# Filter row sums by accumulating transfers, input parts of a convolution in steps, and a projection's first products in other PSUM tiles

## The chip, the cores and the metric

The kernel runs on one core of a Trainium2 chip. The metric is the device time of one execution in microseconds. TensorE (PE) multiplies, with PEld for its weight loads; VectorE (DVE) works elementwise; ScalarE (ACT) applies functions and copies; GpSimd (POOL) does small work and issues DMAs; SyncE (SP) issues DMAs alone.

## The reference

Eight images of 512 channels and 32 x 32 points go through one residual block. All is float32.

```python
def cbs(x, w, p, pad):
    return silu(bn_eval(conv2d(x, w, pad), p))

def bot_attention(x, qkv_w, rw, rh):             # 4 heads of 64 channels, 1024 positions
    q, k, v = conv2d(x, qkv_w, 0) split in three
    logits = einsum('bhdi,bhdj->bhij', q, k + (rw + rh)) * 64 ** -0.5
    return einsum('bhij,bhdj->bhdi', softmax(logits), v)

t = cbs(group_norm(x), cv1_w, cv1_bn, 0)         # 512 -> 512, 32 groups
ys = [t[:, :256], t[:, 256:]]
for i in range(2):
    yi = ys[-1]
    z = cbs(yi, m_cv1_w[i], m_cv1_bn[i], 1)      # 3 x 3, 256 -> 256
    z = bot_attention(z, m_qkv_w[i], m_rw[i], m_rh[i])
    ys.append(yi + silu(bn_eval(conv2d(z, m_cv2_w[i], 0), m_cv2_bn[i])))
out = x + cbs(concatenate(ys), cv2_w, cv2_bn, 0) # 1024 -> 512
```

## The kernel before

**Stages.** The images go through in four pairs (a and b). A pair runs: input tiles and 3 x 3 convolution of module n=0 for both images, projection and attention of a, projection and attention of b, then the same for n=1, then cv2. The group norm and cv1 of the next pair run inside these attentions and between them. Pair 0 has no pair before it: its norm and cv1, and those of image 2, run at the start.

**The 3 x 3 convolution** uses a minimal-filtering (Winograd) scheme with rows and columns transformed apart. `conv3x3` (L585) makes six turns (two output blocks, three row groups i), each with an inner and an outer PSUM tile of the pool `big` (three tiles). VectorE combines them: two instructions form m from the inner tile (L649, L650), one e from the outer tile (L652), and more follow. In the last turn this is done image by image ("parts"), so that part 0's silu comes early. `first_sum` (L872) gives t1 for the projection.

**Filters.** `make_u` (L393) transforms one block of 3 x 3 filters, nine taps of 128 x 128 in `area`, into 18 tiles, in eight steps on VectorE (a generator; every `next` makes a step): for i=2 two column steps; for i=0 a row step (L400 to L402) and two column steps; for i=1 a row step (L404 to L406) and two column steps. ScalarE copies the outer columns, POOL stores the results. The blocks of module 0 are made at the start; those of module 1 in pair 0: one in `early`, in the projection of a, and the others by `step_u` in and around the two attentions. `load_late` brings their taps through POOL's queue into the padded images Y2, which are idle then.

**Input tiles.** `tiles_in` (L513) transforms a padded image for one i in twelve VectorE instructions, with two memsets on POOL for the edges. For n=1 the tiles of image a are made early: i=1 and i=2 by `tiles_later` in attention b of n=0 (i=1 before it in pairs 0 to 2), stored by POOL into `v_dram` and loaded by SP before the convolution.

**Projection.** `project_strassen` (L875) forms q, k and v with seven products instead of eight, each of two q/k matmuls (512 columns) and four for v, into the pools `big` (three tiles) and `av` (one). Fourteen projections use it; seven of them follow a convolution directly, the other seven pass `early` (sums of the attention before). Pair 0's n=0 uses `project_direct` (L827), where VectorE adds the position terms to k from PSUM (L845, L846).

**Attention.** `attention_fast` (L975) takes four groups (channel block, half) of eight key blocks, in pairs. Per pair TensorE makes logits (L998), ScalarE the exponentials (L1002), TensorE the values (L1032), VectorE adds the exponentials up (L1016, L1018) for the sums (L1049). At a group's end ScalarE and VectorE evict the one `av` tile into z (L1039, L1040). Other work hangs on the pairs: `behind` maps a key (group, pair), or the group alone for its pair 0, to functions, which `hooks` builds from norm steps, `step_u` steps and extras. Key (0,3) stands behind the eviction of group 0; the later group ends have no such edge.

**Order.** A planner orders the instructions of each engine: of those that are ready in its model, the one traced first goes first. `tc.issue_after(ins)` puts what is traced under it behind `ins`, on the engine of `ins` alone. Engines and queues are then strictly in order. PSUM dependences are kept by tile: a write to one half waits for a reader of the other.

**Pair 0's extras.** In attention a: twelve `step_u` steps, the position sums of module 1 (`make_r`, L202: a ScalarE turn and four VectorE sums of 128 x 512, each stored by POOL) and the weight sums of its projection (`make_sq`, L234: four sums of 128 x 384 and seven POOL stores). In attention b: eight `step_u` steps and `tiles_later(2)` at (2,1).

Of the kernel before, what the change touches and what calls it, by code (L numbers as in the profile page):

```python
# [61 lines left out]
def kernel(  # L62
# [70 lines left out]

    def load_taps(n, oc, k, area):
        nc.sync.dma_start(
            area[:, : 9 * P].rearrange("p (t o) -> p t o", o=P), m_cv1_w[n, ts(k, P), :, ts(oc, P)]
        )
        return area
# [254 lines left out]
    def make_u(n, oc, k, area, full=None, new=u_new_late, stores=None):  # L393
# [4 lines left out]
        for i in (2, 0, 1):  # L398
            if i == 0:
                tt(mid[:, 1], g0, g2, ALU.add)  # L400
                tt(mid[:, 0], mid[:, 1], g1, ALU.add)
                last = tt(mid[:, 1], mid[:, 1], g1, ALU.subtract)  # L402
            elif i == 1:
                stt(mid[:, 1], g2, 4.0, g0, ALU.mult, ALU.add)  # L404
                stt(mid[:, 0], g1, 2.0, mid[:, 1], ALU.mult, ALU.add)
                last = stt(mid[:, 1], g1, -2.0, mid[:, 1], ALU.mult, ALU.add)  # L406
# [67 lines left out]
    def stages(act, small, ps_big, ps_av, n_pt):  # L474
# [38 lines left out]
        def tiles_in(yp, put, is_=(0, 1, 2), ec=None, room=None, ec_at=("rs", 4)):  # L513
# [17 lines left out]
            for i in is_:  # L531
                ba = g = None
                if i == 0:
                    ba = row_tile("w_ba")
                    stt(ba, rows(1, 2), -4.0, rows(3, 2), ALU.mult, ALU.add)
                elif i == 1:
                    for j in range(2):
                        ec[j] = act.tile([P, NT, NM * F], F32, tag=ec_at[0], name="w_ec", bufs=ec_at[1])
                        tt(ec[j], rows(3 + j)[:, :, 0], rows(1 + j)[:, :, 0], ALU.subtract)
                else:  # L540
                    g = row_tile("w_g")
                    tt(g, rows(0, 2, 5), rows(2, 2), ALU.subtract)
# [6 lines left out]
                if i == 0:  # L549
                    tt(to[0], two(ba[:, :, 1]), two(ba[:, :, 0]), ALU.add)  # L550
                    tt(to[1], two(ba[:, :, 1]), two(ba[:, :, 0]), ALU.subtract)
                elif i == 1:
                    stt(to[0], two(ec[0]), 2.0, two(ec[1]), ALU.mult, ALU.add)
                    stt(to[1], two(ec[0]), -2.0, two(ec[1]), ALU.mult, ALU.add)
                else:
                    stt(to[0], two(ec[1]), 0.25, two(g[:, :, 0]), ALU.mult, ALU.add)
                    stt(to[1], two(ec[0]), -4.0, two(g[:, :, 1]), ALU.mult, ALU.add)
# [14 lines left out]
                tt(d_of(2), cols(M0 + 1, M1 - M0), cols(M2, M3 - M2), ALU.subtract)  # L572
# [3 lines left out]
                stt(v34[:, 1], d[:, 1], -2.0, d[:, 2], ALU.mult, ALU.add)  # L576
# [5 lines left out]
                last = tt(v12[:, 1], a, b, ALU.subtract)  # L582
            return last

        def conv3x3(n, vs, u_of, z, groups=G, summed=None, after=None, between={}):  # L585
# [10 lines left out]
            for oc in range(NM):  # L596
                dst = z[:, oc].rearrange("p g x -> p (g x)").rearrange("p (t r w) -> p r t w", r=4, w=F)
                for i in range(NI):
# [44 lines left out]
                    m_t = m.rearrange("p r a q -> p (r a q)")  # L643
                    for part in range(parts):
                        qs, tl, xs_ = ts(part, n_q), ts(part, n_q // NT), ts(part, 4 * n_q)
                        m = m_t.rearrange("p (g r a q) -> p g r a q", a=4, **by_part)[:, part]
                        e = e_t.rearrange("p (g r a q) -> p g r a q", a=2, **by_part)[:, part]
                        r = r_t.rearrange("p (g r t x s) -> p g r t x s", g=parts, r=2, x=4, s=NT)[:, part]
                        tt(m[:, :, 0::2], slots(inner_ps, 0)[..., qs], m24[..., qs], ALU.add)  # L649
                        tt(m[:, :, 1::2], slots(inner_ps, 0)[..., qs], m24[..., qs], ALU.subtract)  # L650
# [224 lines left out]
        def project_strassen(n, z, w, t, early=None, middle=None):  # L875
# [10 lines left out]
            def product(ps, v, w, rhs, onto=False, between=None):  # L886
# [4 lines left out]
                if between:  # L891
                    between()
                for j in range(HALF // P):
# [3 lines left out]
                    )  # L897

# [18 lines left out]
            ps_a, ps_b, ps_v = big(), big(), ps_av.tile([P, 2, HALF], F32, tag="av", name="pv_ps")  # L917
# [3 lines left out]
            product(ps_a, ps_v[:, 0], w["11"], b11, between=early)  # L921
            nc.scalar.copy(u, ps_a)
            nc.scalar.copy(u_v, ps_v[:, 0])
            product(ps_b, ps_v[:, 1], w["s1"], t1)
            nc.scalar.copy(m5, ps_b)  # L925
# [644 lines left out]
    chunk = make_u(0, 0, 0, areas[0, 0, 0], first_units)  # L1570
# [19 lines left out]
    chunk = make_u(0, 0, 1, areas[0, 0, 1], first_units, stores=first_stores)  # L1590
# [9 lines left out]
    with tc.issue_after(made.ins), tc.issue_after(powered.ins):  # L1600
        nc.vector.tensor_scalar(rstd, bnp[:, :, 3], BN_EPS, None, ALU.add)
        nc.gpsimd.tensor_tensor(rstd, rstd, mhalf[:, :NBN], ALU.pow)
# [13 lines left out]
    norm = s.group_norm_part(xs_second, by_act=NX - 1, behind=behind_u)  # L1616
# [78 lines left out]

    def third_norm(done):
        with tc.issue_after(last.ins), tc.issue_after(s.silued[0].ins), tc.issue_after(done.ins):
            next(norm)

    def third_parts(done):  # L1700
        for g in range(G):
            s.tiles_in(Y1[g], putter(vs, g), [2], ecs[g])

# [9 lines left out]
    for p in range(NP):  # L1713
# [57 lines left out]
        def load_late(oc, k, area):  # L1771
            nc.gpsimd.dma_start(
                area[:, : 9 * P].rearrange("p (t o) -> p t o", o=P), m_cv1_w[1, ts(k, P), :, ts(oc, P)]
            )
            return area

# [5 lines left out]
        if p == 0:  # L1782
            with tc.issue_after(powered.ins):
                first_taps, second_taps = [load_late(0, k, inside(Y2[k])) for k in range(NM)]
# [19 lines left out]
        if direct:  # L1804

            def early():
                with tc.issue_after(s.silued[0].ins):
                    for _ in make_u(1, 0, 0, first_taps, new=u_new_early):
# [43 lines left out]
        if p == 0:  # L1852
            more_u = filters([(0, 1, second_taps), (1, 0, load_late(1, 0, inside(Y2[0])))])
            late_taps = []
# [4 lines left out]
            extra = {key: lambda: next(r_steps) for key in ((0, 3), (1, 1), (1, 3), (2, 1), (2, 3))}  # L1859
            extra[2, 2] = lambda: late_taps.append(load_late(1, 1, inside(Y2[1])))  # L1860
            
            def with_sq():
                with tc.issue_after(put_r[0].ins):
                    make_sq(1, q_tiles, [t[:, j] for t in q_sums for j in range(2)])

            extra[3, 2] = with_sq
        behind = hooks(() if p == 0 else NORM_A, {i: 1 for i in range(12)}, extra) | {NG: begin_cv1(0, Y1[0], ia + 2)}
# [41 lines left out]
        else:  # L1909
# [11 lines left out]
            if direct:  # L1921
                m2_a()
                end.check()
                with tc.issue_after(s.m2_silu[0].ins):
# [297 lines left out]
```

## Time and profile before

| | us |
|---|---|
| three runs | 2284.47, 2286.85, 2290.32 (median 2286.85) |
| profiled execution | 2286.45, of which the span is 2284.6 |
| PE / DVE / ACT / POOL busy in the span | 2218.8 / 1753.0 / 1097.9 / 204.7 |
| mean granted TensorE clock | 0.993 |
| moved by DMA | 281.06 MB, 123 GB/s |

The span runs from the first instruction to the last. A wait is the idle time of an engine ahead of an instruction, put down to what released it: "who <- whom: us in total, times, longest". A row of a stage gives its bounds in us, its length, the busy time (and number of instructions) of the engines, the granted clock, and the share and rate of DMA.

### The profile page before, as it was taken

Reading aid. Unit: us, or ns where it says so; the run is one execution under the profiler, and the core shown is the slowest. Engines: PE = TensorE matmul, PEld = TensorE weight load, DVE = VectorE, ACT = ScalarE, POOL = GpSimd, SP = SyncE. Lnnn points to the kernel's source line nnn. Section 1 sums busy time; section 2 is a strip of 40 time slices with the busy share of each in tenths; the row PEclk is TensorE's granted clock in tenths of the full one; section 3 lists DMA queues with packets and bytes.
Section 4 is the critical chain, followed back from the end, with each engine's and each line's share of the span. In section 5 each row is a group of like instructions: output and inputs, shape, how many; then the busy total and the mean of one; then the engine's idle time right before and its main releaser. Section 6 shows DMA issues by size and latency. Waiting matters only on the chain.

```text
span 2284.6 us, 40531 instructions
## 1 busy us (share of the span) xinstructions
PE 2218.8 (97%) x16338; PEld 1081.3 (47%) x16338; DVE 1753.0 (77%) x2701; ACT 1097.9 (48%) x1361; POOL 204.7 (9%) x409
## 2 busy tenths in 40 slices
PE   7999999999999999999999999999999999999997
PEld 3653437343474444734447343654345643473443
DVE  7988789878668689886857868986784868886742
ACT  7454553554225665366324666455622455336533
POOL 2212010000220000000021000000012000000002
PEclk9999999999999999999999999999999999999999
DMA  7835247321572323612267151532137611251115
GB/s 256 297 127 192 75 140 261 108 74 57 138 241 86 106 90 107 206 53 75 56 162 254 32 176 33 176 118 77 55 80 180 215 53 46 69 195 43 47 29 135
DMA packets 128420, 281.06 MB, mean 123 GB/s; under 512 B 34112, under 2 KB 56364, under 8 KB 127200
## 3 DMA queue, kind: packets, MB, share of 16 engines
q1 hardware_dynamic: 100240, 192.25, 25.7%
q0 software_dynamic: 27984, 86.13, 12.6%
q8 instruction: 131, 2.15, 0.4%
q14 instruction: 65, 0.53, 0.1%
HBM read 210.29 MB, written 68.03 MB: 122 GB/s over the span
## 4 chain that ended last, share of the span: by engine, by line


## 5 line engine op out<-in xcount | busy, mean ns | idle before, releaser
L1002 ACT ACTIVATE pt<-l_ps 128x1024 f32<-128x1024 f32 x512 | 495.6, 1023 | 363.1 <-PE l_ps L998 332.7
L1018 DVE TENSOR_TENSOR acc<-acc,pt 128x1024 f32<-128x1024 f32 x384 | 469.8, 1223 | 94.2 <-ACT pt L1002 71.9
L1032 PE MATMUL av_ps<-pt,vT 64*64 64x512 f32 x4096 | 491.3, 597 | 15.1 <-DVE z L1040 14.8
L998 PE MATMUL l_ps<-q,kr 64*64 64x512 f32 x4096 | 487.2, 592 | 1.7 <-ACT pt L1002 0.8
L1032 PEld LDWEIGHTS av_ps<-pt,vT 64*64 64x64 f32 x4096 | 155.8, 134 | 291.2 <-issue 240.0
L998 PEld LDWEIGHTS l_ps<-q,kr 64*64 64x64 f32 x4096 | 158.5, 134 | 274.5 <-issue 253.5
L628 PEld LDWEIGHTS c_ps<-v_in,u 128*64 128x64 f32 x4320 | 235.7, 137 | 5.3 <-issue 5.3
L628 PE MATMUL c_ps<-v_in,u 128*64 128x128 f32 x4320 | 237.5, 273 | 0.0
L1231 PE MATMUL m_ps<-z,m_sb 128*128 128x512 f32 x256 | 112.8, 593 | 0.4 <-DVE z L1104 0.4
L633 ACT COPY c_m<-c_ps 128x512 f32<-128x512 f32 x48 | 28.2, 587 | 175.9 <-PE c_ps L628 130.3
L888 PE MATMUL p_ps<-t_z,sq 128*128 128x512 f32 x224 | 108.1, 602 | 3.2 <-DVE c_t L650 3.2
L1016 DVE TENSOR_TENSOR acc<-pt 128x1024 f32<-128x1024 f32 x64 | 78.0, 1218 | 34.3 <-ACT pt L1002 34.3
L478 ACT ACTIVATE t<-m_ps,bh,sh 128x512 f32<-128x512 f32 x64 | 46.4, 775 | 87.8 <-PE m_ps L1231 87.8
L888 PE MATMUL p_ps<-z,sq 128*128 128x512 f32 x168 | 80.8, 604 | 0.2 <-ACT m_z L925 0.2
L1301 POOL DMA_DIRECT2D c_out<-in_x_dram x56 | 49.9, 975 | 310.1 <-ACT c_out L478 307.8
L1231 PEld LDWEIGHTS m_ps<-z,m_sb 128*128 128x128 f32 x256 | 48.2, 190 | 59.6 <-issue 56.4
L1104 DVE TENSOR_TENSOR z<-z,rs 128x512 f32<-128x512 f32 x64 | 43.9, 686 | 23.6 <-DMA rs<-r_dram 23.1
L478 ACT ACTIVATE c_out<-cz,bh,sh 128x512 f32<-128x512 f32 x14 | 16.7, 1295 | 90.3 <-DVE cz L1328 90.3
L1040 DVE TENSOR_TENSOR z<-av_ps,z 128x512 f32<-128x512 f32 x64 | 44.0, 688 | 19.5 <-ACT z L1039 19.5
L478 ACT ACTIVATE z<-z,bh,sh 128x512 f32<-128x512 f32 x64 | 47.7, 805 | 22.0 <-DVE z L677 22.0
L888 PEld LDWEIGHTS p_ps<-t_z,sq 128*128 128x128 f32 x224 | 39.2, 192 | 35.8 <-issue 35.8
L1351 PE MATMUL x_ps<-t_x,sw 128*128 128x512 f32 x128 | 55.9, 592 | 0.0
(308 smaller groups left out, 3163.1 us busy)
## 6 DMA issues: line engine op xcount, KB each, us to landing
u<-u SPq DMA_DIRECT2D x135, 512.0 KB
sq<-sq SPq DMA_DIRECT2D x42, 384.0 KB
rs<-r_dram SPq DMA_DIRECT2D x118, 128.0 KB
x<-in_x_dram SPq DMA_DIRECT2D x28, 512.0 KB
r_in<-r SPq DMA_DIRECT2D x28, 512.0 KB
y_in<-y SPq DMA_DIRECT2D x28, 512.0 KB
c_out<-in_x_dram POOLq DMA_DIRECT2D x56, 256.0 KB, 5.4
out_dram<-c_out POOLq DMA_DIRECT2D x56, 256.0 KB, 3.8
```

Of the source, the lines that this page charges most:

```text
L478: silued[0] = nc.scalar.activation(dst, src, AF.Silu, scale=sh[:, k : k + 1], bias=bh[:, k : k + 1])
L628: conv_product[0] = nc.tensor.matmul(to[o], us[cp][:, k, row, c, o], rhs, start=(k == 0), stop=(k == NM - 1),)
L888: nc.tensor.matmul(ps[:, o, :], w[:, o, :], rhs, start=not onto, stop=True, skip_group_check=onto)
L998: nc.tensor.matmul(ps[kh * HD : (kh + 1) * HD, hd, :], kr[r, c, o : o + HD], q[r, c, ts(half, HALF)], start=True, stop=True,)
L1002: last_exp[0] = exp = nc.scalar.activation(pt, ps, AF.Exp, scale=SCALE)
L1016: return nc.vector.tensor_tensor(accs[g], pt[0], pt[1], ALU.add)
L1018: ins = nc.vector.tensor_tensor(accs[g], accs[g], pt[i], ALU.add)
L1032: nc.tensor.matmul(avs[g][hd * HD : (hd + 1) * HD, kh, :], vT[r, j, o : o + HD], pt[i][r, hd, :], start=(j == 0), stop=(j == NJ - 1),)
L1040: evicted[0] = nc.vector.tensor_tensor(dst, av[:, 1], dst, ALU.add)
L1231: nc.tensor.matmul(pss[half][:, oc, :], m2_sb[:, n, k, ts(oc, P)], ao[:, k, ts(half, HALF)], start=(k == 0), stop=(k == NM - 1),)
L1301: nc.gpsimd.dma_start(t, rows_of(x, i, at), accum_op=ALU.add)
L1351: nc.tensor.matmul(ps[:, o, :], w[:, c, ts(o, P)], rhs[c], start=(c == 0 and not onto), stop=(c == 1), skip_group_check=onto,)
```

## The change

- `make_u` takes a switch `summed`. With it (all but the first two blocks), g0+g1+g2 of a block's taps is expected in the area's rows 9 to 11, and i=0's row step is one instruction in place of three. The sum is made by DMA: `load_row` brings tap row r there, row 0 plainly, rows 1 and 2 with `accum_op=ALU.add`. For the two blocks (0,1,k), row 0 goes through SP and rows 1 and 2 through POOL, behind the power of `rstd`. For module 1, `load_late` issues taps and three rows on POOL; its first two calls move from before the first convolution to the hook `third_parts` in it, behind the power of the third image's statistics.
- The statistics of image 1's fourth chunk are made by ScalarE instead of VectorE (`by_act=NX`).
- `tiles_in` becomes a generator of five pieces (`tiles_steps`). In attention b of n=0 a piece each is made at (1,3), (2,1), (2,3), 3 and (3,2); in pair 3 the ten pieces of i=1 and i=2 are made at the keys (g,1) to (g,3).
- In the last turn of `conv3x3` the m instructions of both parts come before the rest.
- In `project_strassen` ps_b is the `av` tile and ps_v a `big` tile; both q/k products come first, then the two v products, and the copies in another order.
- In pair 0, attention a keeps ten `step_u` steps and the ScalarE turn; the four position sums, the weight sums and five steps of block (1,1) come behind m2 of image a, before the projection of b. Attention b keeps three steps.

```diff
+    def load_row(n, oc, k, area, r, q=None, **kw):
+        (q or nc.gpsimd).dma_start(
+            area[:, 9 * P : 12 * P].rearrange("p (t o) -> p t o", o=P),
+            m_cv1_w[n, ts(k, P), 3 * r : 3 * r + 3, ts(oc, P)], **kw
+        )
...
             if i == 0:
-                tt(mid[:, 1], g0, g2, ALU.add)
-                tt(mid[:, 0], mid[:, 1], g1, ALU.add)
-                last = tt(mid[:, 1], mid[:, 1], g1, ALU.subtract)
+                if summed:
+                    last = stt(mid[:, 1], g1, -2.0, mid[:, 0], ALU.mult, ALU.add)
...
+                    for part in range(parts):
+                        qs, m = ts(part, n_q), m_parts[:, part]
+                        tt(m[:, :, 0::2], slots(inner_ps, 0)[..., qs], m24[..., qs], ALU.add)
+                        tt(m[:, :, 1::2], slots(inner_ps, 0)[..., qs], m24[..., qs], ALU.subtract)
                     for part in range(parts):
...
-            ps_a, ps_b, ps_v = big(), big(), ps_av.tile([P, 2, HALF], F32, tag="av", name="pv_ps")
+            ps_a, ps_b, ps_v = big(), ps_av.tile([P, 2, HALF], F32, tag="av", name="p_ps"), big()
...
-            product(ps_a, ps_v[:, 0], w["11"], b11, between=early)
+            to_qk(ps_a, w["11"], b11)
+            if early:
+                early()
+            to_qk(ps_b, w["s1"], t1)
+            to_v(ps_v[:, 0], w["11"], b11)
             nc.scalar.copy(u, ps_a)
+            nc.scalar.copy(m5, ps_b)
+            to_v(ps_v[:, 1], w["s1"], t1)
             nc.scalar.copy(u_v, ps_v[:, 0])
-            product(ps_b, ps_v[:, 1], w["s1"], t1)
-            nc.scalar.copy(m5, ps_b)
             nc.scalar.copy(m5_v, ps_v[:, 1])
...
+        scaled = nc.gpsimd.tensor_tensor(rstd, rstd, mhalf[:, :NBN], ALU.pow)
+        with tc.issue_after(scaled.ins):
+            for r in (1, 2):
+                for k in range(NM):
+                    load_row(0, 1, k, areas[0, 1, k], r, accum_op=ALU.add)
...
-    norm = s.group_norm_part(xs_second, by_act=NX - 1, behind=behind_u)
+    norm = s.group_norm_part(xs_second, by_act=NX, behind=behind_u)
...
+        for r in range(3):
+            load_row(1, oc, k, area, r, **({"accum_op": ALU.add} if r else {}))
...
+        with tc.issue_after(after_norm[0].ins):
+            late_taps.extend(load_late(0, k, inside(Y2[k])) for k in range(NM))
...
-            extra = {key: lambda: next(r_steps) for key in ((0, 3), (1, 1), (1, 3), (2, 1), (2, 3))}
-            extra[2, 2] = lambda: late_taps.append(load_late(1, 1, inside(Y2[1])))
...
+            extra = {
+                (2, 2): lambda: late_taps.append(load_late(1, 1, inside(Y2[1]))), (3, 1): lambda: next(r_steps),
+            }
+        behind = hooks(() if p == 0 else NORM_A, {0: 2} | {i: 1 for i in range(1, 9)}, extra) | {NG: begin_cv1(0, Y1[0], ia + 2)}
...
-                m2_a()
+                last = m2_a()
                 end.check()
+                with tc.issue_after(last.ins):
+                    for _ in r_steps:
+                        pass
+                    with tc.issue_after(put_r[0].ins):
+                        make_sq(1, q_tiles, [t[:, j] for t in q_sums for j in range(2)])
+                more_u = filters([(1, 1, late_taps[2])])
+                with tc.issue_after(last.ins):
+                    for _ in range(5):
+                        step_u()
...
+        parts_at = iter(())
+        if more:
+            parts_at = tiles_later(2)
+        else:
+            parts_at = (part for i in (1, 2) for part in tiles_later(i))
...
+        at_keys = ((1, 3), (2, 1), (2, 3), 3, (3, 2)) if more else [(g, at) if at else g for g in range(NG) for at in range(1, 4)]
+        behind = hooks(NORM_B, {0: 1, 1: 1, 4: 1}, {key: step_part for key in at_keys}) | {
...
-        apply = behind[2, 1]
-        behind[2, 1] = lambda: (apply(), tiles_later(2))
```

## The prediction

> **What bounds the kernel now.** I read the page's busy times first, then TensorE's waits, then each attention as a stage of its own, then single stalls on the timeline.
>
> ```profile
> span 2284.6 us, 40531 instructions
> PE 2218.8 (97%) x16338; PEld 1081.3 (47%) x16338; DVE 1753.0 (77%) x2701; ACT 1097.9 (48%) x1361; POOL 204.7 (9%) x409
> PE av_ps L1032 <- DVE z L1040: 14.8, 12, 3.1
> PE s_ps L1049 <- DVE acc L1018: 8.0, 6, 2.1
> PE gm_ps L697 <- DVE mv L691: 7.9, 1, 7.9
> PE c_ps L628 <- DVE v_in L581: 5.0, 2, 4.8
> PE pv_ps L894 <- ACT u_zv L923: 4.8, 7, 0.7
> PE p_ps L888 <- DVE c_t L650: 3.2, 7, 1.1
> ```
>
> TensorE is the bound, and no edit removes a matmul. So the change can win only TensorE's idle time, 65.8 us, and what idling does to its clock. The waits say where 44 us of that lie: on VectorE inside attention (22.8), at the start (12.9, of which the first 7.9 is loading), and at the start of a projection (8.0).
>
> The stages next: each row is one attention: bounds, length, busy time of PE, PEld, DVE, ACT, POOL, granted clock.
>
> ```profile
> 146.56:207.82 61.26, 55.82 (x509) 19.17 (x512) 53.54 (x79) 36.21 (x50) 13.83 (x25) 0.97 0.33 112
> 253.84:314.93 61.09, 56.22 (x517) 19.94 (x520) 53.98 (x81) 39.25 (x50) 10.73 (x18) 0.97 0.31 102
> 815.50:873.92 58.42, 56.00 (x517) 20.42 (x520) 50.33 (x68) 36.71 (x43) 3.17 (x6) 0.97 0.13 43
> 1369.43:1427.65 58.22, 55.80 (x517) 20.20 (x520) 50.11 (x67) 36.59 (x43) 3.18 (x6) 0.97 0.11 35
> 1896.81:1955.86 59.05, 54.20 (x509) 18.79 (x512) 53.11 (x70) 32.67 (x37) 3.48 (x8) 1.00 0.15 52
> 2129.71:2183.63 53.92, 53.92 (x509) 18.74 (x512) 41.45 (x45) 32.45 (x37) 0.00 (x0) 1.00 0.05 15
> ```
>
> The last row carries no foreign work: 53.92 us, no idle, VectorE free for 12.5 us, 3.1 us in each of the four groups. The five above are exactly the n=0 attentions whose hooks the change touches: 7.34, 7.17, 4.50, 4.30 and 5.13 us over 53.92, 28.4 us together. A test of "3.1 per group": in the first row's second group the hooks put four filter steps (4.8 us) and two position sums of 0.69 on VectorE, 6.2 us; less 3.1 leaves 3.1, and the longest av_ps wait is 3.1.
>
> **The clock: row against rule.** PE busy in four of those rows is 1.9 to 2.3 us above 53.92, at clock 0.97. The timeline of one:
>
> ```profile
> 863.48 0.64 PE L1049 MATMUL s_ps<-acc,ones 128*32 128x256 f32 x8 [1.42 <-DVE acc L1018]
> 865.12 3.13 PE L1032 MATMUL av_ps<-pt,vT 64*64 64x512 f32 x16 [1.00 <-DVE z L1040]
> ```
>
> Two short idles, then sixteen matmuls take 3.13 us instead of 1.90: the clock was halved. The Trainium skill, "TensorE: Matmul & The Clock Gate", Part 1, has the clock fall only after an idle window of about 3.4 us; its last table tells authors to avoid idles above 3 us. By the rule this stall costs 2.4 us; by the row about 4.4. The row decides: removing a stall of 2 to 3 us is worth up to two microseconds more, 8.2 us over the four rows, which the rule would not count.
>
> **Part 1, attention (likeliest -21.1).** A late z eviction (L1040) holds TensorE at a group's end; about 1 us of lateness is absorbed.
> - Pair 0, image a: the position sums leave, ten filter steps instead of twelve stay, one row step shrinks from 1.7 us (0.55 + 0.56 + 0.56, L400 to L402) to one instruction of 0.56. Group 1 gets steps of 1.0, 1.0, 0.56, 1.0 (0.5 over the slack); group 2 gets 1.0, 1.7, 1.0, 1.0 (1.6 over). Less the tolerated 1: a stall of 1.1, rounded up to 1.3. 61.26 to 55.2: -6.1.
> - Pair 0, image b: three filter steps (3.7 us) instead of eight (9.7), and the block of twelve input instructions (6.6 us) in five pieces of about 1.3. Statistics of 1.5 us at two keys stay. Stalls of about 1.4 remain, because pieces at keys (1,3) and (2,3) can stand in front of an eviction. 61.09 to 55.3: -5.8.
> - Pairs 1 and 2, image b: the same five pieces at keys two pairs apart, where two pairs give 1.6 us of slack. The stalls shown above go with their clock dip; the 0.55 at the end stays and 0.5 is new. To 55.0: -3.4 and -3.2.
> - Pair 3, image b: ten pieces, 13.2 us, against 12.5 of slack. Spreading cannot make room; about 2.5 us of stall stay. To 56.5: -2.6.
>
> Bounds: all stalls gone, -28.4; half of them merely moved, -12.
>
> **Part 2, projection (-7.4).** Seven projections follow a convolution directly:
>
> ```profile
> 387.81 1.05 PE L894 MATMUL pv_ps<-sq,z 128*128 128x128 f32 x8
> 389.56 0.94 PE L894 MATMUL pv_ps<-sq,t_z 128*128 128x128 f32 x6 [0.70 <-ACT u_zv L923]
> 390.70 1.96 PE L888 MATMUL p_ps<-t_z,sq 128*128 128x512 f32 x4 [0.21 <-DVE c_t L650]
> ```
>
> The second v product waits until ScalarE has copied the first out of the same PSUM tile, and ps_b waits for the convolution's last PSUM tile. In the new order both q/k products run first (ps_b sits in the idle av tile), then both v products with no copy traced between them; and the convolution's final m sums for both images come first, so the tile that ps_v inherits is free after L650 of part 1, some 1.5 us sooner (the six part-0 instructions it overtakes). What is late next is part 0's silu, pushed back 0.7 us by the two m instructions now ahead of it; it is due about when TensorE wants it. Five places at 0.8: 4.0. At 945 us the waits are 0.68 and 1.13 with four matmuls stretched from 1.96 to 3.31: 3.2, less 0.5 because t1 (L872) ends after the first product, less 0.5 for the silu: 2.2. At 1499 us, 1.8 less 0.6: 1.2. Projections with `early` show no wait now; the av tile they need must be evicted at the same point as before: 0. Bounds: -3 (ScalarE's order goes against it) and -9.5.
>
> **Part 3, the start (-0.8).** The convolution waits 4.77 us at 76 us for VectorE, and its first 64 matmuls then run at half clock. Off VectorE come one chunk's statistics (1.28 + 0.21) and 1.1 in each of two filter blocks. But ScalarE gets the chunk: a sum of 1.25 us that fits its idle 1.41 at 31 us, and a square pass, +1.15 at 38 us. TensorE's statistics matmul is due at 38.9, the new mv at about 39.3: all later steps slip 0.5, and VectorE, which already waits there, loses its 1.5. Only the second block's 1.1 lies behind that point; with 0.2 for the first it is 1.3 less 0.5. Bounds: +2 and -6.9 (4.77 plus 2.1 of half clock). The four accumulates are issued from 26.3 us, while the DMA engines stand at share 0.01 from 32 to 37 us: the sum is there by about 36, when wanted.
>
> **Part 4, what moves behind m2 of image a (+2.3).** Position sums (4 x 0.6), the weight sums (4 x 0.47) and five filter steps (4.7): 9.0 us on VectorE, traced ahead of the projection's k additions. Cover: VectorE is idle for 4.6 us only later.
>
> ```profile
> 236.74 1.22 DVE L845 TENSOR_TENSOR kr<-ps,rw_sb 128x1024 f32<-128x1024 f32 x1 [1.26 <-PE ps L505]
> 250.52 1.23 DVE L845 TENSOR_TENSOR kr<-ps,rw_sb 128x1024 f32<-128x1024 f32 x1 [4.62 <-PE ps L505]
> ```
>
> If they run as traced, from 235.5, L845 starts at 244.5 and ends at 245.8, and it holds one of three big PSUM tiles that the second v product wants at 243.5: TensorE waits 2.3. The two more filter steps before m2 (1.5 us) fit VectorE's 4.65 us idle at 216 to 220. Bounds: 0 (fitted between) and +5 (with a clock dip). On the queues: eleven POOL stores (0.54 to 0.78 each) move to where POOL idles 23 us; SP is not touched.
>
> **Part 5, the accumulating rows (+1.0).** Six blocks get three row transfers each: two on SP, sixteen on POOL, 0.54 to 0.98 each, some 14 us on a queue that is busy 9%; 3.5 MB on 281. No row shows an accumulate of 192 KB; the nearest is c_out, 256 KB, 5.4 us to landing (4.1 to 10.2). Rows of one block wait for one another, and POOL, in order, waits with them: 11 us a block by that row, 5 us by the formula of the skill's page "DMA: Bandwidth & Descriptors", section "Anatomy of one DMA" (2.0 + bytes/436e3, an estimate of 2.45 each). I take the row. The first two blocks are loaded after the third statistics' power (L717, done at 84.7 us) instead of at 77 us, and their sums are wanted by VectorE at about 135, so 22 us of chain or even 44 fit. But beside the chain in pair 0's first convolution stand the memsets for the input tiles (89.3 and 94.0 us), which VectorE needs. Lower bound 0 (planned behind them), upper in the rival below; I put 1.0.
>
> Sum: -21.1 - 7.4 - 0.8 + 2.3 + 1.0 = -26.0 against the profiled execution, 2286.45 us: 2260.5. The median of the runs is 0.4 higher: 2261.
>
> **Rivals.**
> - *VectorE stays the bound of these attentions* (0.14). The work is moved, not removed (8 us less in all), and pieces in front of evictions stall as blocks did. For: 50 to 54 us busy in four rows. Against: an attention at 964 us has 47.45 busy and no idle. Part 1 then gives -9, the rest as above: 2273.
> - *The POOL chain holds VectorE* (0.07, slower). Before, the loads issued at 77 us took 14.5 and 16.7 us to land, with DMA share at 1.0 until 90. Two blocks with two waits each, at 10 to 15 us, keep POOL until 125 to 145; if the planner put the memset of 94 us behind them, the convolution waits some 40 us: 2261 + 40 = 2301. It decides above 26 us past 94 us. Against: memsets are traced ahead of the loads, and DMA share is 0.25 from 95 us.
> - *The gains are met by the losses* (0.05): part 4 at +5 with a dip, part 1 and 2 at their low ends, two memset waits: 2284.
> - My forecast: 0.74.
>
> 2250 takes in all stalls gone at half the start's bound; 2277 the first rival with its own spread. About 7 us (0.3%) is what a measurement can tell from no change: faster 0.74 + 0.14 = 0.88, same 0.05, slower 0.07.
>
> **What would show it.** Right: the five attentions at 55 to 56.5 us, the u_zv wait gone, half-clock windows at 183, 306, 866, 948 and 1419 us gone, a new wait of some 2 us before L858 near 240 us, av_ps waits of about 1 us left at group ends. Wrong: a POOL wait "<-DMA" with a VectorE wait on a memset at 95 to 130 us, or attentions still at 58 and more.

## The result and the profile after

| | us |
|---|---|
| before, median of 21 runs | 2286.61 (2283.22 to 2290.32) |
| after, median of 21 runs | 2280.59 (2277.58 to 2286.69) |
| ratio | 0.9977, interval 0.997 to 0.9984 |
| after, profiled execution | 2278.14, of which the span is 2276.4 |

The change wins 6 us where 26 were forecast. First the attentions that the prediction showed, in the same order and the same columns (bounds and length; busy time and count of PE, PEld, DVE, ACT, POOL; granted clock; DMA share and rate):

```profile
157.97:220.91 62.94, 57.29 (x509) 18.70 (x512) 45.91 (x63) 37.03 (x49) 13.93 (x20) 0.95 0.33 86
266.93:322.24 55.31, 54.29 (x517) 19.94 (x520) 48.02 (x67) 38.21 (x46) 7.08 (x10) 1.00 0.31 107
820.83:875.58 54.75, 54.29 (x517) 19.93 (x520) 48.38 (x63) 36.49 (x43) 2.64 (x5) 1.00 0.10 33
1369.35:1424.10 54.75, 54.29 (x517) 19.94 (x520) 48.38 (x63) 36.49 (x43) 2.63 (x5) 1.00 0.11 34
1891.07:1946.80 55.73, 54.12 (x509) 18.74 (x512) 51.47 (x65) 32.45 (x37) 2.93 (x7) 1.00 0.16 51
```

Four of the five rows stand where the forecast put them (55.3, 55.0, 55.0, 56.5). The first does not: it is 1.7 us longer than before, although VectorE has 7.6 us less to do in it, and its clock is 0.95. It also begins 11.4 us later than before, at 157.97 instead of 146.56. Read like this, the table names two places at once: something ahead of attention a, and something in it. TensorE's waits say what kind:

```profile
PE c_ps L645 <- DVE v_in L599: 12.5, 2, 6.9
PE l_ps L1026 <- ACT pt L1030: 6.0, 5, 4.5
PE av_ps L1060 <- DVE z L1068: 6.0, 13, 1.1
PE p_ps L908 <- ACT z L488: 2.5, 7, 0.5
PE s_ps L1094 <- DVE acc L1046: 2.1, 3, 1.0
PE p_ps L908 <- ACT m_z L951: 2.0, 2, 1.0
PE p_ps L908 <- DVE t_z L892: 1.1, 2, 0.6
```

The waits at group ends (av_ps, and s_ps of the sums) have fallen from over 22 us to 8, as forecast, and the one for u_zv is almost gone. New are 7.5 us for the convolution's tiles and 4.5 us for logits in one piece. I followed each backward.

**Place 1, pair 0's convolution.** POOL's queue (start, duration, engine, line, operation; in brackets the idle time ahead and what ended it):

```profile
87.55 0.80 POOL L135 DMA_DIRECT2D ypad<-in_m_cv_w_dram  x1
...
94.64 1.30 POOL L135 DMA_DIRECT2D ypad<-in_m_cv_w_dram  x1 [4.49 <-DMA ypad<-in_m_cv_w_dram]
95.43 0.68 POOL L561 MEMSET w_rows<- 128x32 f32 x1
95.49 0.68 POOL L562 MEMSET w_rows<- 128x32 f32 x1
98.88 1.27 POOL L135 DMA_DIRECT2D ypad<-in_m_cv_w_dram  x1 [2.71 <-DMA ypad<-in_m_cv_w_dram]
100.90 1.26 POOL L135 DMA_DIRECT2D ypad<-in_m_cv_w_dram  x1 [0.75 <-DMA ypad<-in_m_cv_w_dram]
104.47 1.25 POOL L135 DMA_DIRECT2D ypad<-in_m_cv_w_dram  x1 [2.31 <-DMA ypad<-in_m_cv_w_dram]
105.25 0.64 POOL L561 MEMSET w_rows<- 128x32 f32 x1
```

An accumulating row (1.25 to 1.30 us) waits for the row before it to land, and the memsets of the input tiles stand in the queue behind such waits. The second pair of memsets comes at 105.25; before, it waited for VectorE alone:

```profile
93.96 0.16 POOL L544 MEMSET w_rows<- 128x32 f32 x1 [4.46 <-DVE w_ab L579]
```

In the changed kernel VectorE waits 3.25 us for the first pair and 3.53 for the second, and TensorE behind it:

```profile
105.92 0.69 DVE L589 TENSOR_TENSOR w_d<-w_rows 128x512 f32<-128x512 f32 x1 [3.53 <-POOL w_rows L561]
```

```profile
110.15 5.12 PE L645 MATMUL c_ps<-v_in,u_new 128*64 128x128 f32 x54 [6.91 <-DVE v_in L599]
```

The clock fell to half 4.1 us into the 6.91 us of idling (at 107.37) and stayed there for 6.8 us. From its first matmul to its last in c_ps the convolution takes 55.05 us (78.23 to 133.28) instead of 45.89 (76.47 to 122.36).

**Place 2, attention a.** VectorE, then TensorE:

```profile
168.99 0.56 DVE L408 SCALAR_TENSOR_TENSOR ypad<-ypad 128x384 f32<-128x384 f32 x1 [11.86 <-DMA ypad<-in_m_cv_w_dram]
169.46 1.22 DVE L1044 TENSOR_TENSOR acc<-pt 128x1024 f32<-128x1024 f32 x1
```

```profile
180.01 1.99 PE L1026 MATMUL l_ps<-q,kr 64*64 64x512 f32 x8 [4.50 <-ACT pt L1030]
182.94 3.38 PE L1060 MATMUL av_ps<-pt,vT 64*64 64x512 f32 x16
```

L408 is the row step of block (1,0) of module 1, the fifth of the six blocks with row sums (below: the fifth block), and the first of its steps that reads the sums. It was planned ahead of attention's first add, L1044. POOL's queue shows the three rows that it waits for:

```profile
153.61 0.78 POOL L135 DMA_DIRECT2D ypad<-in_m_cv_w_dram  x1
160.47 1.31 POOL L135 DMA_DIRECT2D ypad<-in_m_cv_w_dram  x1 [6.07 <-DMA ypad<-in_m_cv_w_dram]
164.83 1.28 POOL L135 DMA_DIRECT2D ypad<-in_m_cv_w_dram  x1 [3.05 <-DMA ypad<-in_m_cv_w_dram]
```

The last one landed 4.1 us after its issue, at 168.9. Until then VectorE sits for 11.86 us, and all that stands behind L408 is late. ScalarE waits for it twice:

```profile
170.77 1.94 ACT L1030 ACTIVATE pt<-l_ps 128x1024 f32<-128x1024 f32 x2 [3.58 <-DVE acc L1044]
178.32 0.42 ACT L426 ACTIVATE u_new<-ypad 128x256 f32<-128x256 f32 x1 [5.61 <-DVE ypad L408]
```

The first wait is for the add, which lets a buffer of the exponentials go. The second is for the row step of another filter block, which VectorE reached only at 177.74: ScalarE's copy for that block (L426) stands in its queue ahead of the next exponentials. These come at 178.94, and TensorE has stood 4.50 us for them, two steps removed from the cause. The clock fell to half 3.5 us into that idling (at 179.05), and sixteen matmuls take 3.38 us instead of 1.90. "<-DMA" at the head of a VectorE line with a long bracket is the line to look for; TensorE's own list only names ScalarE.

**Place 3, the start.** The same L408 waits there for the sums of the two blocks (0,1,0) and (0,1,1) of module 0:

```profile
37.66 0.56 DVE L408 SCALAR_TENSOR_TENSOR taps<-taps 128x384 f32<-128x384 f32 x1 [3.24 <-DMA taps<-in_m_cv_w_dram]
45.28 0.56 DVE L408 SCALAR_TENSOR_TENSOR taps<-taps 128x384 f32<-128x384 f32 x1 [1.98 <-DMA taps<-in_m_cv_w_dram]
```

The theory to test: the accumulating rows, put at 1.0 us, cost some 20, by order at three places and not by bytes. Rivals: the traffic of the rows, VectorE's new order, or parts 1, 2 and 4 that bring less than they seem to.

### The profile page after: what moved, and what is told of

The parts are those of the page before. It is cut to its first block, busy times and chain, and to the rows that moved or that the text cites. A ratio compares the mean times of both kernels' runs of the same rounds, so it can differ in the third digit from the quotient of the medians.

```text
span 2276.4 us, 40540 instructions
## 1 busy us (share of the span) xinstructions
PE 2214.4 (97%) x16338; PEld 1081.6 (48%) x16338; DVE 1744.6 (77%) x2686; ACT 1103.5 (48%) x1367; POOL 225.7 (10%) x425
## 4 chain that ended last, share of the span: by engine, by line
PE 67%; DVE 18%; issue 7%; DMA 4%; ACT 3%; POOL 1%; SPq 0%; DVEq 0%; POOLq 0%; ACTq 0%
PE av_ps L1060 15%; PE l_ps L1026 14%; PE c L1279 9%; PE c_new L1279 6%; PE ps L515 5%; PE p_ps L908 5%; PE m_ps L1259 4%; PE c_ps L645 3%; DVE acc L1046 2%; PE p_ps L914 2%; PE x_ps L1379 2%; PE s_ps L1077 1%; DMA taps<-in_m_cv_w_dram 1%; DVE c_e L672 1%; DMA ypad<-in_m_cv_w_dram 1%
## 5 line engine op out<-in xcount | busy, mean ns | idle before, releaser
L1044 DVE TENSOR_TENSOR acc<-pt 128x1024 f32<-128x1024 f32 x64 | 78.0, 1219 | 34.0 <-ACT pt L1030 34.0
L1259 PEld LDWEIGHTS m_ps<-z,m_sb 128*128 128x128 f32 x256 | 48.3, 190 | 58.8 <-issue 56.2
L1067 ACT COPY z<-av_ps 128x512 f32<-128x512 f32 x64 | 37.5, 585 | 34.6 <-PE av_ps L1060 34.6
```

Of the source, the lines that this page charges most:

```text
L1044: return nc.vector.tensor_tensor(accs[g], pt[0], pt[1], ALU.add)
L1259: nc.tensor.matmul(pss[half][:, oc, :], m2_sb[:, n, k, ts(oc, P)], ao[:, k, ts(half, HALF)], start=(k == 0), stop=(k == NM - 1),)
```

## The experiments

Times are medians; the ratio is to the kernel before, run on the same chip beside it. A kernel whose time is 2287 has ratio 1. "The kernel without sums" is e1_no_sums.

**Without the accumulating rows.** All row loads go, and VectorE forms the sums with three operations again.

```diff
-def make_u(n, oc, k, area, ..., summed=True):
+def make_u(n, oc, k, area, ..., summed=False):
-        load_row(n, oc, k, area, 0, nc.sync)        # in load_taps
-        for r in range(3): load_row(1, oc, k, ...)  # in load_late
-        with tc.issue_after(scaled.ins): ...load_row(0, 1, k, areas[0, 1, k], r, accum_op=ALU.add)
```

> The changed kernel with its filter sums back on VectorE (three operations a block) and no accumulating row loads at all; the other three parts as changed. Theory (the chains of accumulating rows cost at three places: about 2.6 us at the start, 9.7 us in pair 0's convolution by POOL's memsets, 7.7 us in attention a of pair 0 by VectorE's wait for the sums): the convolution ends about 147 to 148 us as before, attention a takes about 55.5 us, the whole about 2281 - 20 = 2261 us (2257 to 2265). Rival 1 (the row loads cost nothing, the loss is VectorE's new order of work or the moved steps): attention a stays at 62 to 63 us, the convolution's end stays near 158 us, the whole 2279 to 2284. Rival 2 (the sums on VectorE cost about what the rows cost): the stalls go but the three added operations a block bring back most of it, 2272 to 2278.

Measured: 2263.8 us (ratio 0.9899, 0.9886 to 0.9911). From the profiled executions, after less this: start of the convolution 78.23 - 77.04 = 1.2; the convolution 55.05 - 46.53 = 8.5; attention a 62.94 - 57.04 = 5.9; everything behind, -1.5. The theory holds, with a smaller loss at each place than it expected; both rivals fall. The start's 1.2 us is no more than the scatter found below. Attention a of this kernel, and the stretch from there to attention b:

```profile
148.25:205.29 57.04, 54.23 (x509) 18.65 (x512) 49.18 (x68) 37.16 (x49) 7.72 (x15) 1.00 0.24 77
205.29:251.30 46.01, 46.01 (x152) 22.25 (x145) 38.08 (x67) 18.18 (x28) 14.27 (x27) 1.00 0.72 244
```

VectorE is busy 3.3 us longer in attention a than in the changed kernel, mostly because it forms the sums itself, and the attention is 5.9 us shorter. The work was cheaper than the wait that replaced it.

**Rows behind the memsets.** All loads and all bytes stay; two rows each of two blocks are ordered behind the last memset.

```diff
-            late_taps.extend(load_late(0, k, inside(Y2[k])) for k in range(NM))
+            late_taps.extend(load_late(0, k, inside(Y2[k]), sums=False) for k in range(NM))
+            with tc.issue_after(s.cleared[0].ins):      # the last memset of the tiles
+                for k in range(NM):
+                    add_rows(0, k, late_taps[k])        # rows 1 and 2, accumulating
```

> The changed kernel with only the four accumulating rows of pair 0's convolution (image blocks (0,0) and (0,1) of the second stage) put behind the last memset of the convolution's input tiles on POOL's queue; the taps and first rows are loaded where they were. Theory (POOL waits for an earlier row's landing with the memsets behind it, VectorE waits 3.25 and 3.53 us for these, and the matmuls stand 6.91 us and then run 6.8 us at half the clock): the convolution ends 9 to 10 us sooner, the wait for c_ps at 110 us and the half-clock window at 107 us are gone, attention a keeps its 62.9 us; the whole about 2271 (2269 to 2273). Rival (the order of POOL's queue is harmless there; VectorE's added parts or the traffic of the rows held the convolution): within 2 us of the changed kernel, 2279 to 2282.

Measured: 2270.98 us (0.9936, 0.9921 to 0.9951). POOL again:

```profile
96.55 0.16 POOL L563 MEMSET w_rows<- 128x32 f32 x1 [4.45 <-DVE w_ab L599]
96.61 0.17 POOL L564 MEMSET w_rows<- 128x32 f32 x1
97.10 1.31 POOL L135 DMA_DIRECT2D ypad<-in_m_cv_w_dram  x1 [0.33 <-issue]
```

The memsets wait for VectorE alone, the convolution takes 46.53 us (78.42 to 124.95), as without sums, and attention a is still slow at 62.71. Since the bytes are the same, it was the order of the queue.

**Left-over steps later.** The other place alone.

```diff
+        with tc.issue_after(end.adds[9].ins) if p == 0 else nullcontext():
             while step_u():
                 pass
```

> The changed kernel with only the left-over filter steps of attention a of pair 0 ordered behind the tenth pair's add on VectorE, so that the row step that reads the sums of block (1,0) no longer stands ahead of attention's first add. Theory (VectorE waited 11.86 us there for the last accumulating row, the first products with v stood 4.50 us, and a half-clock window followed): attention a falls from 62.9 us to 55 to 56 us, the convolution stays as changed (end near 158 us), the whole about 2273 (2271 to 2275). Rival (attention a is slow for the transfers' traffic or the moved steps, not for VectorE's wait): attention a stays over 61 us, the whole 2279 to 2282. Between: the stall goes but the half-clock window comes at another place, 2276 to 2278.

Measured: 2270.73 us (0.9926, 0.9914 to 0.9939), a little better than expected. The row of attention a:

```profile
159.31:215.59 56.28, 54.22 (x509) 18.65 (x512) 45.95 (x63) 37.47 (x49) 13.90 (x20) 1.00 0.37 97
```

VectorE's busy time is that of the changed kernel (45.95 against 45.91), as are the transfers; 6.7 us went with the position of one block's left-over steps, of which the first, an instruction of 0.56 us, is the one that had waited. The clock is back at 1.00. The convolution stays slow (55.5 us).

**Both.**

> The changed kernel with both edits: the convolution's accumulating rows behind the last memset, and the left-over filter steps behind the tenth pair's add. Theory: the two gains are at different places and add up, 2281 - 9.6 - 7.5 = 2264 us (2260 to 2267), with only the start's loss of about 2.6 us against the kernel without row sums left, so that kernel and this one lie within 3 us. Rival (one stall hides the other, or the rows moved later hold the projection's early filter steps instead): 2268 to 2274.

Measured: 2264.9 us (0.9906, 0.9891 to 0.992). The two edits together give 15.7 us of the 16.8 that leaving the rows out gives. With the rows well placed, the kernel is no faster than without rows: 4.8 us less work on VectorE (1745.1 busy against 1749.9) buy nothing that these runs can show. By stages the two differ: attentions a and b of pair 0 are 0.8 and 1.0 us shorter with the rows, and the convolution begins 2.5 us later (79.52 against 77.04). The shorter attentions need not be the rows' doing, since the kernel with the old order of m, below, has them without rows. No run has the rows of module 1, well placed, without those at the start, so whether the sums could win in that form is open.

**The rows alone, on the kernel before.** Only the part with the sums is applied.

```diff
 def load_taps(...):
+        load_row(n, oc, k, area, 0, nc.sync)
 def load_late(...):
+            for r in range(3): load_row(1, oc, k, area, r, **({"accum_op": ALU.add} if r else {}))
# and the row step of one instruction, and the rows behind the power of rstd, as in the change
```

> The kernel before with the accumulating row sums alone: the rows of two blocks at the start, of the two blocks loaded in pair 0's convolution, and of the two loaded from attention a on; everything else as before. POOL's order puts two of the convolution's accumulating rows ahead of a memset of the input tiles, as in the changed kernel; the row step of block (1,0) stands behind an add in the middle of attention a. Theory (the chains cost at the start and in the convolution, and nothing is paid back): start +1 to +2 us, convolution +9 to +10, attention a 0 to +1: 2287 + 11 = 2298 us (2294 to 2301). Rival (the row sums lighten VectorE, and only together with the parts in steps do they harm): 2283 to 2288.

Measured: 2296.89 us (1.0043, 1.003 to 1.0057): slower, and the total is as the theory has it. By stages the start loses 2.5 us and the convolution 12.9, more than expected, and attention a wins 1.8 (59.51 against 61.26): with more of VectorE's work in attention a, as in the kernel before, the lighter filter steps seem to pay something back. The loads stand at the old place, and a second victim appears behind them:

```profile
92.80 1.30 POOL L135 DMA_DIRECT2D ypad<-in_m_cv_w_dram  x1 [9.58 <-DMA ypad<-in_m_cv_w_dram]
93.62 1.56 POOL L727 TENSOR_TENSOR gr<-gr,mhalf 128x4 f32<-128x4 f32 x1
...
102.80 1.27 POOL L135 DMA_DIRECT2D ypad<-in_m_cv_w_dram  x1 [4.50 <-DMA ypad<-in_m_cv_w_dram]
103.57 0.67 POOL L554 MEMSET w_rows<- 128x32 f32 x1
```

```profile
95.41 2.23 ACT L769 ACTIVATE x<-x,shift,gr 128x512 f32<-128x512 f32 x3 [9.56 <-DVE shift L763]
```

The third norm's power (L727) waits on POOL, so does ScalarE's normalising (the second fence, ScalarE's line), and TensorE stands 5.4 us for x. The changed kernel loads behind that power and so avoids this one, not the memsets. The convolution is 58.8 us long here.

**The start's rows alone**, put back into the kernel without sums.

```diff
-    chunk = make_u(0, 1, 0, areas[0, 1, 0], ..., summed=False)
+    chunk = make_u(0, 1, 0, areas[0, 1, 0], ..., summed=True)     # and (0, 1, 1), with their rows
```

> The kernel without row sums (2263.8 us), with the accumulating rows of the two blocks at the start alone put back. Theory (VectorE waits about 3.2 us for the sums at 37 us, and the convolution begins 1.2 us later, 78.2 against 77.0): the convolution begins at 78 to 79.5 us, the whole 2265.5 us (2264.5 to 2267). Rival (the start's difference is the scatter of one execution): 77 us, 2263 to 2264.5.

Measured: 2267.08 us (0.9911, 0.9896 to 0.9926); the convolution begins at 78.75. The ratios of the two kernels overlap, so the total does not decide, and 2.4 us of it lie in attention a of n=1, whose code is the same, with a half-clock window at 447 us. The stage speaks for the theory, over several kernels with the same start: with these rows it began at 78.2, 78.4, 79.1, 79.5 and 78.75; without them at 77.0, 76.9, 76.9, 77.0 and once 78.1. That is about 1.7 us between the medians, with a scatter of 1.2 to 1.3 in either group.

**Undoing the other parts, one at a time, from the kernel without sums.** Whole input parts:

```diff
-        behind = hooks(NORM_B, {...}, {key: step_part for key in at_keys})
+        behind = hooks(NORM_B, {...})
+        behind[2, 1] = lambda: (apply(), tiles_whole(2))   # in pair 3 also tiles_whole(1) at (1, 1)
```

> The kernel without row sums (2263.8 us), with one more part undone: the next convolution's input parts are computed whole at one place in each attention b again, not in steps over several places. Theory (the steps alone brought pairs 1 to 3 their 3.66, 3.46 and 3.3 us, and some 3 us of pair 0's attention b): attentions b of pairs 1 to 3 go back to 58.2 to 59.1 us, pair 0's b to 58 to 60 us, attentions a stay; the whole 2263.8 + 10.4 + 3 = 2277 us (2274 to 2280). Rival (the gain came from the moved filter steps and the freed PSUM tiles): 2264 to 2268.

Measured: 2275.72 us (0.9958, 0.9945 to 0.9972), 12 us more. The rows of attentions b of pairs 1 to 3:

```profile
810.78:867.49 56.71, 54.29 (x517) 19.96 (x520) 49.99 (x67) 36.70 (x43) 3.17 (x6) 1.00 0.11 37
1361.03:1417.74 56.71, 54.29 (x517) 19.96 (x520) 49.98 (x67) 36.59 (x43) 3.16 (x6) 1.00 0.11 37
1884.84:1945.58 60.74, 55.90 (x509) 19.24 (x512) 53.09 (x70) 32.68 (x37) 3.47 (x8) 0.97 0.15 50
```

The steps are worth 2.0, 2.0 and 5.0 us there, and 4.3 in pair 0. Pairs 1 and 2 did not go back to the 58.2 to 58.4 of before: the missing 1.6 us are the clock (1.00 here, 0.97 there). The clock dip follows the stall often, not always.

The projection's tiles and order, with the order of m:

```diff
-            ps_a, ps_b, ps_v = big(), ps_av.tile(...), big()
+            ps_a, ps_b, ps_v = big(), big(), ps_av.tile(...)
-            to_qk(ps_a, ...); early(); to_qk(ps_b, ...); to_v(ps_v[:, 0], ...)
+            product(ps_a, ps_v[:, 0], ..., between=early); copies; product(ps_b, ps_v[:, 1], ...)
# and the order of m, as in the next cut
```

> The kernel without row sums (2263.8 us), with one more part undone: the Strassen projection's first products in their old PSUM tiles and order, and the convolution's m of both parts each in its own part again. Theory (the projections' stages were 5.5 us shorter in sum): the waits of TensorE for u_zv (0.7 us, seven times) and for c_t (3.2 us in seven waits) come back, those for z and m_z go; the whole 2269.3 us (2267 to 2271). Rival (these waits were hidden or only traded for others and the 5.5 us came with the other parts): 2262.5 to 2265.

Measured: 2264.65 us (0.9908, 0.9893 to 0.9923): no difference. The theory falls. The waits did change, as expected:

```profile
PE pv_ps L911 <- ACT u_zv L940: 4.8, 7, 0.7
PE p_ps L905 <- DVE c_t L665: 3.5, 7, 1.3
```

These 8.3 us stand against new ones of the kernel without sums, for z 2.5, m_z 2.0, u_zv 1.3 and t_z 1.1, together 6.9. By stages, the stretches with a projection are 3.6 us shorter in sum with the new tiles and order, and pair 0's first projection and two attentions 2.7 us longer.

Only the order of m:

```diff
-        for part in range(parts): m of this part      # both m first
-        for part in range(parts): e, r, silu of this part
+        for part in range(parts): m, e, r, silu of this part
```

> The kernel without row sums (2263.8 us), with only the convolution's m of both parts back in its own part each; the projection's first products stay in their new tiles. Undoing both brought no difference (2264.65 us): the later projections lost 3.5 us, and pair 0's first projection and its two attentions won 2.7 us. Theory (the order of m moves the filter steps on VectorE in pair 0, which costs there, and the new tiles win in the later projections): attention a of pair 0 55.8 us, attention b 54.8 us, the later projections stay near those of the kernel without row sums; the whole 2261.5 us (2260 to 2263). Rival (the order of m is what wins in the later projections, by c_t): these lose about 2 us or more, the whole 2263 to 2266.

Measured: 2265.72 us (0.9908, 0.9893 to 0.9923). Attention a is 55.97 and b 54.75, as the theory has it, but the stretches with a projection lose 3.5 us in sum, as the rival has it. The wait for u_zv has become one for the convolution:

```profile
PE p_ps L911 <- DVE c_t L665: 7.4, 7, 1.2
```

The new tiles need the new order of m; the two together are worth nothing measurable on the whole.

The moved steps back into the attentions:

```diff
-            with tc.issue_after(last.ins):            # behind m2 of image a
-                position sums, projection sums, five filter steps
+            extra = {key: lambda: next(r_steps) for key in ((0, 3), (1, 1), (1, 3), (2, 1), (2, 3))}
+            extra[3, 2] = with_sq                      # and hooks of 12 and 8 filter steps
```

> The kernel without row sums (2263.8 us), with one more part undone: the first pair's position sums, projection sums and filter steps are back inside its two attentions instead of behind the second product of image a. Theory (VectorE sets the pace in attention a and b of pair 0 when it has this work there, and has room between them: 38.1 us busy of 46.0): attention a goes from 57.0 to 60 to 61.5 us, attention b from 55.8 to 57 to 60 us, the stretch between them stays 46.0 us because TensorE fills it either way; the whole 2270 us (2268 to 2274). Rival (the forecast's 2.3 us of waiting in that stretch for the moved work is real but covered): the stretch shrinks to under 45 us and the whole is 2266 to 2269.

Measured: 2278.88 us (0.9961, 0.9948 to 0.9975), 15 us more, over twice what was expected.

```profile
149.30:211.81 62.51, 56.06 (x509) 19.10 (x512) 53.53 (x79) 37.48 (x51) 13.85 (x25) 0.97 0.32 109
211.80:257.82 46.02, 46.02 (x153) 22.24 (x145) 29.48 (x47) 16.28 (x22) 6.14 (x13) 1.00 0.51 183
257.82:315.24 57.42, 54.67 (x517) 19.66 (x520) 51.31 (x76) 39.14 (x50) 8.10 (x14) 1.00 0.21 72
```

Attention a loses 5.5 us, b 1.7, and the stretch behind b 3.1, with two new waits of TensorE for z: 10.2 us that belong to the moved steps. Attention a of n=1 loses 2.3, but with a half-clock window (at 457 us) and a loss like those of the kernel with the start's rows alone, whose code there is unchanged: this can't be put down to the steps. The stretch between a and b is 46.02 in either case, since TensorE is busy for all of it: moving 8.6 us of VectorE's work in there was free. The start is 1.1 us later, within its scatter. Another 3.9 us of the profiled difference lie in the last pair and the end, whose code is the same; the profiled execution is 2.1 us above the median, and I don't count them.

**Two attempts at the start and at a better version.**

```diff
-    norm = s.group_norm_part(xs_second, by_act=NX, behind=behind_u)
+    norm = s.group_norm_part(xs_second, by_act=NX - 1, behind=behind_u)
```

> The kernel without row sums (2263.8 us), with the second image's group-norm share back as before: one of its four statistics on VectorE instead of all four on ScalarE. Theory (the start's forecast of -0.8 us was wrong: ScalarE's later x_second costs TensorE 0.5 us and the statistics another 0.3 us, and the convolution begins at 77.0 us against 76.5 before): the convolution begins at 76.3 to 76.8 us, the whole 2263.2 us (2262 to 2264.5). Rival (the moved statistics help VectorE as forecast and only the profiled executions differ): the convolution begins at 77.5 to 78 us, 2264 to 2265.

Measured: 2265.08 us (0.9908, 0.9892 to 0.9923); the convolution begins at 78.57. The theory falls; the rival's mark is passed by half a microsecond. But VectorE waited 1.07 us for a filter store in this execution, and the kernel before, with the same share, began at 76.47. The next kernel, with the old share too, began at 79.11. Both lie above all five starts with the new share and no rows (76.9 to 78.1), which leans the rival's way; what the share is worth stays open within some 2 us.

Put together from three of these edits (group-norm share and order of m as before, left-over steps behind the tenth add, no sums):

> A version put together from what the runs showed: no row sums, input parts in steps, first pair's steps moved, projection's first products in new tiles; group-norm share and order of m as before, and the left-over filter steps of attention a behind the tenth pair's add. Theory (gains of 0.6 at the start and 2 to 3 in pair 0 add up): 2260.5 us (2258.5 to 2262.5). Rival (these are shifts of VectorE's order that give back elsewhere): 2263 to 2265.

Measured: 2268.15 us (0.9919, 0.9905 to 0.9932), a miss: the start came at 79.11 and the later projections lost their 3.6 us; attention a at 55.76 could not pay for both. The kernel without sums, 2263.8 us, remains the best, 16.8 below the changed kernel.

## Why the prediction was wrong, point by point

- **Part 5 (+1.0) is the step that failed.** It measured about 15.6 us in three stages (1.2 + 8.5 + 5.9), 14.0 over the whole profiled execution and 16.8 by the medians. The length of a chain was not the error: in attention a POOL needed 11.2 us from the fifth block's plain row to the issue of its last one (153.61 to 164.83), the 11 that was taken from the row of c_out. A single accumulating row took 4.0 to 7.0 us to land, where the row of c_out gave 5.4 and the estimate by the Trainium skill, "DMA: Bandwidth & Descriptors", section "Anatomy of one DMA", 2.45. The error was where the chain stands. "Memsets are traced ahead of the loads" does not fix a queue: before, the memsets came at 89 and 94 us, when VectorE had freed their buffers. The row transfers wait for no such thing, so by the planner's rule (of those that are ready, the one traced first) they could go in front. That is what the queue shows; the planner's reason is inferred. And the consumer was looked at for four blocks of six. For two, "wanted at about 135" held: the rows had landed by 109 us. At the start "the sum is there by about 36, when wanted" was wrong by 1.6 us for the first block (37.6) and by 9 for the second (45.3). At the fifth block nothing was said, and there VectorE itself waited.
- **The second rival had the mechanism.** Its sign of being right, a POOL wait "<-DMA" with a VectorE wait on a memset at 95 to 130 us, is there word for word. Its price was not: 8.5 us instead of 40, because the four accumulating rows ahead of the memset were through POOL by 105 us, and not by 125 to 145. It was weighed as a case of its own that outdoes all gains; at its measured price it is a loss beside them, and a little over half of what the rows cost.
- **Part 1 (-21.1) was right** once the rows are out: without the sums the five attentions fall by 4.2, 5.3, 3.7, 3.5 and 3.3 us, 20.0. (Half of 28.4 is 14.2; the bound of -12 does not follow from it.) Undoing the parts shows both halves: steps 13.3 us over the four attentions b, moved work 5.5 and 1.7 in pair 0.
- **The row against the clock rule was right in direction.** The dips named at 306, 866, 948 and 1419 us are gone. The one at 183 us is gone without the sums; the changed kernel has a longer one there, in the stall of Place 2. But the dip is not certain: one execution of the sums alone had the same old attention b at both clocks:

```profile
828.21:884.92 56.71, 54.30 (x517) 19.96 (x520) 50.31 (x68) 36.70 (x43) 4.16 (x6) 1.00 0.13 44
1379.12:1437.53 58.41, 55.99 (x517) 20.42 (x520) 50.09 (x67) 36.58 (x43) 3.16 (x6) 0.97 0.11 35
```

1.7 us with the dip, none without, at the same 2.4 us of idling. In the two new stalls of the change, 6.91 and 4.50 us, the clock fell 4.1 and 3.5 us into the idling and stayed at half for 6.8 us each; there the rule of the Trainium skill, "TensorE: Matmul & The Clock Gate", Part 1, which wants an idle window of about 3.4 us, agrees.
- **Part 2 (-7.4) was mis-sized.** "It is due about when TensorE wants it" was said of part 0's silu: the wait for it is 2.5 us over seven projections. Two of the seven also got a wait of 1.0 us for m_z, which the forecast did not have. Against the kernel with the old products and order of m, the stretches of these seven are 5.1 us shorter. Those with `early`, put at 0, are 1.5 us longer, with waits for u_zv of 1.1 and 0.2 us. What was left, 3.6 us, did not show on the whole, since pair 0's first projection and two attentions lost 2.7.
- **Part 3 (-0.8)** is not contradicted and not shown: the start's scatter is larger.
- **Part 4 (+2.3) measured 0**: the stretch stayed 46.02 us, with TensorE busy throughout. The low bound, "fitted between", was the case.

In sum, by the profiled executions: without the rows -22.3 us (2264.14 against 2286.45) where the forecast's other parts gave -27.0; the rows +14.0 (2278.14) where it gave +1.0.

## What to carry to other kernels

A transfer that waits for an earlier one is a wait on the queue of the engine that issues it: list what else stands on that queue, and who waits for each of these, before counting what the transfer saves. Ask for every consumer when the data lands, and pin a consumer that could be planned too early behind an instruction of its own engine; here one block's left-over steps, the first of them 0.56 us long, in a wrong place cost over 6. Where the work stands counted for more than how much there is: spreading VectorE's work within four attentions brought 13.3 us there, moving some to a stretch that TensorE fills brought 7.1 in the two attentions that it left, and removing 5 us of it by transfers brought nothing on the whole.

## What the hardware showed unexpectedly

In the changed kernel an accumulating row of 192 KB keeps POOL 1.25 to 1.31 us for the issue in ten of twelve cases (1.48 and 1.78 at the start), a plain one 0.78 to 0.80; and POOL's busy time rose by 21 us (204.7 to 225.7), where some 14 were put. To landing the two differ little: in a quiet stretch, from 197 us, a plain row took 4.0 us and the two accumulating ones behind it 4.3 and 4.1. A memset of 128x32 takes 0.15 to 0.17 us after an idle, and shows 0.64 to 0.68 behind an accumulating row, whose own record it overlaps. The same old attention b ran at 56.7 or 58.4 us, by the granted clock alone.
